# The last two blocks' attention divided in SBUF, and late outputs that sum their experts in one bank

## The chip, the core and the metric

The kernel runs on one core of one Trainium2 chip. The metric is the device time of one execution in microseconds, and the median of three executions stands for a kernel. Beside them there is one profiled execution, whose trace gives the time of every instruction. The engines are called PE (matmuls; PEld is its weight load), DVE (vector), ACT (scalar activation), POOL (GpSimd) and SP, which here only issues DMA transfers. Each engine works its own queue of instructions strictly in the order in which the program put them there.

## What is computed

The input is four images of 128 channels and 64x64 pixels, that is 4 x 4096 tokens of 128 channels. Two layers follow one another. The first normalises, convolves, runs a Mamba scan (16 states for each of 4 x 4 channel groups) and projects. The second is what the change is about:

```python
def _L1_attn_ref(x, W_qkv, b_qkv, W_proj, b_proj):
    # E = 128 channels, H = 4 heads of D = 32
    ...
    scores = jnp.einsum('bhnd,bhmd->bhnm', q, k) * scale
    att = jax.nn.softmax(scores, axis=-1)
    out = jnp.einsum('bhnm,bhmd->bhnd', att, v)
    out = jnp.transpose(out, (0, 2, 1, 3)).reshape(b, n, e)
    return out @ W_proj + b_proj

def _L1_ffn_ref(x, router_w, router_b, expert_w, expert_b):
    # E = 8 experts, K = 2 of them for each token
    router_probs = jax.nn.softmax(x @ router_w + router_b, axis=-1)
    top_p, top_i = jax.lax.top_k(router_probs, K)
    top_p = top_p / jnp.sum(top_p, axis=-1, keepdims=True)
    expert_out = jnp.einsum('bnd,edc->bnec', x, expert_w) + expert_b
    gathered = jnp.take_along_axis(expert_out, top_i[..., None], axis=2)
    return jnp.einsum('bnk,bnkc->bnc', top_p, gathered)

t = t + _L1_attn_ref(_ln_t(t), ...)
t = t + _L1_ffn_ref(_ln_t(t), ...)
```

## The kernel before

The work is cut into blocks of 512 tokens, eight for each of the four images. The program is one long loop over slots (from line 1362). Each pair of slots of the first 1024 takes one unit of the scan; `END` (line 1340) is the slot behind the last unit. In every slot there is also one step of attention, called a group, if one is ready: four score matmuls, two exponentials on ACT, and, one slot later, eight matmul calls that add the weighted values to the bank `av` (`weighted`, line 981). A matmul of fp32 operands is recorded twice in the trace.

Attention goes by pairs of blocks of queries: `q` is a pair, `u` one block of it. For each head `h` of a pair all keys of the image are run through, in pieces that `RUNS` (line 903) orders; the last piece of every image is the whole of pair 3. When the last group of a head's piece is done, `avs` takes the bank out to SBUF (a copy on ACT, or an addition of `prev`, the partial sum of earlier pieces, on DVE). It holds two blocks: partitions 64u to 64u+31 are the head's 32 output channels, not yet divided, and partitions 64u+32 to 64u+63 repeat the softmax denominator.

If the head is final, `avs` is sent to the DRAM tensor `total` (line 1007). Behind the fourth head `inverted` (line 1012) loads the denominators of all heads as `den`, 128x32, takes the reciprocal, and sends it to the DRAM tensor `inverse`; then it queues two tasks "out", one for each block. These three steps come 4, 6 and 8 slots after the fourth head.

A task "out" is `finished` (line 1032), a generator that does the rest of a block. Each `yield` ends one stage. It loads `aT` (the undivided attention, four heads on 128 partitions), `inv` (the reciprocals, repeated for the 32 channels of a head) and `acc` (the block's residual) from DRAM, multiplies aT by inv on DVE (line 1047), projects with `wp` on PE, adds to `acc`, takes the norm's statistics, transposes, computes the routing with some 20 small DVE instructions, and sends the shares of the eight experts to DRAM as `shares`. From there `share` (line 1117) loads them again, two experts at a time, repeated over all partitions. DVE multiplies the tokens by the shares and PE multiplies by the experts' weights. The bias of the experts and each two experts make a bank of their own; DVE adds it to `res` in SBUF (lines 1134, 1145 and 1152), so that there are five additions for one block.

Two lanes of such tasks, X and Y, run beside attention. `advance` (line 1254) carries a lane on by one stage; in a slot the calls come in the order X, Y, Y, X, the last X behind `weighted`. Up to `END` lane Y prepares the scan's blocks and lane X does the closing of blocks and the outputs. From `END` on lane Y takes outputs from lane X's list as well (line 1261), so they go in pairs. Each lane has one PSUM bank. `send` (line 422) issues a transfer some slots later on SP. All engine instructions of the loop go through `queued` (line 389), which chains them in program order; for this reason every profile line reads L406, and groups are told apart by the tiles they name.

Of the kernel before, what the change touches and what calls it, by code (L numbers as in the profile page):

```python
# [9 lines left out]
F32 = mybir.dt.float32  # L10
# [7 lines left out]
P = 128  # L18
C = 128
EPS = 1e-5  # L20
BLK = 512
# [4 lines left out]
DH = 32  # L26
NH = 4
NE = 8
# [8 lines left out]
def conv_mamba_attn_moe_kernel(ctx: ExitStack, tc: tile.TileContext, t: dict):  # L37
    nc = tc.nc
    x, out = t["x"], t["out"]
    B, _, L = x.shape  # L40
    NB = L // BLK
# [41 lines left out]
    wv, wp, rw, ew, eb8 = (load(k, eng=late) for k in ("wv", "wp", "rw", "ew", "eb8"))  # L83
# [13 lines left out]
    for j in range(4):  # L97
        r = slice(DI * (j % 2), DI * (j % 2) + DI)
# [301 lines left out]
    class Queue:  # L400
# [7 lines left out]
    tensor, vector, scalar, gpsimd, sync = (  # L408
        Queue(e) for e in (nc.tensor, nc.vector, nc.scalar, nc.gpsimd, nc.sync)
    )  # L410

    def mm(out, lhsT, rhs, start=True, stop=True):
        tensor.matmul(out, lhsT=lhsT, rhs=rhs, start=start, stop=stop)
# [8 lines left out]
    def send(out, in_, slots=1):  # L422
        outgoing.append([slots, out, in_])
# [19 lines left out]
    att, mix, side = pool("att"), pool("mix"), pool("side")  # L443
# [4 lines left out]
    def work(lane, shape=None):  # L448
        return ps_work.tile(shape or [P, BLK], F32, tag=f"work{lane}", name=f"ps_{lane}")

    def tmp(lane, name, shape=None):
        return side.tile(
            shape or [P, BLK], F32, tag=f"tmp{lane}", name=name, bufs=6 if lane == "X" else 4
        )
# [516 lines left out]
    sums, partial, total, inverse, later = [None], {}, {}, {}, deque()  # L971
# [9 lines left out]
    def weighted(group):  # L981
        b, q, h, pTs, first, last, prev, final = group
        if first:
            sums[0] = ps_av.tile([P, BLK], F32, name="av")
        av = sums[0]
        for k, (v, pT) in enumerate(pTs):
            for u in range(2):
                mm(
                    av[64 * u : 64 * u + 2 * DH, :], v, pT[:, u, :],
                    first and k == 0, last and k == STEP - 1,  # L990
                )
        if last:
            avs = att.tile([P, BLK], F32, name="avs", bufs=2)
            if prev is None:
                scalar.copy(avs, av)
            else:
                vector.tensor_add(avs, av, prev)


            if not final:  # L1000
                partial[b, q, h] = dram.tile([P, BLK], F32, name=f"avd{q}{h}")
                send(partial[b, q, h], avs, 3)
                return
            if h == 0:
                total[b, q] = dram.tile([2, 2, NH, DH, BLK], F32, name=f"total{q}")
            d = total[b, q]
            send(d[:, :, h].rearrange("u k r q -> (u k) r q"), avs, 3)
            if h == NH - 1:
                work_left = inverted(b, q)
                later.extend((slot + n, work_left) for n in (4, 6, 8))  # L1010

    def inverted(b, q):

# [15 lines left out]
            ))  # L1029
        yield  # L1030

    def finished(b, qb, lane):

        q, u = divmod(qb, 2)
        td = kqv[b][3]
        s = slice(qb * BLK, (qb + 1) * BLK)
        acc = side.tile([P, NT, C], F32, name="acc", bufs=2)
        aT, inv = tmp(lane, "aT"), tmp(lane, "inv")
        sync.dma_start(out=aT, in_=total[b, q][u, 0].rearrange("h d q -> (h d) q"))
        sync.dma_start(  # L1040
            out=inv, in_=inverse[b, q][u][:, None, :].to_broadcast([NH, DH, BLK])
        )
        sync.dma_start(out=acc.rearrange("p j c -> p (j c)"), in_=td[:, s])
        yield
        yield
        yield
        vector.tensor_mul(aT, aT, inv)
        yield
        ps = work(lane, [P, NT, C])
        for j in range(NT):  # L1050
            mm(ps[:, j, :], aT[:, j * P : (j + 1) * P], wp)
        yield
        vector.tensor_add(acc, ps, acc)
        rs = spread(lane, acc)
        yield
        ps = transposed(lane, acc)
        yield
        xf = tmp(lane, "xf")
        scalar.copy(xf, ps)
        yield  # L1060
        ps = work(lane, [P, NT, NE])
        for j in range(NT):
            mm(ps[:, j, :], xf[:, j * P : (j + 1) * P], rw)
        wide = [P, NT, NE]

        def routed(name, n=NE):
            return small.tile([P, NT, n], F32, name=f"{name}{lane}", bufs=1)

        yield

        both = routed("both", 2 * NE)
        pr = routed("pr")
        vector.tensor_mul(pr, ps, rs[:, :, None].to_broadcast(wide))
        vector.tensor_add(pr, pr, rb[:, None, :].to_broadcast(wide))
        m = routed("m", 1)
        vector.tensor_reduce(m, pr, AX.X, ALU.max)
        vector.tensor_sub(pr, pr, m.to_broadcast(wide))
        yield
        yield
        scalar.activation(pr, pr, AF.Exp)  # L1080
        yield
        yield

        revb = rev[:, None, :].to_broadcast(wide)

        def largest(src, tag):
            top, f, pick = routed(f"top{tag}", 1), routed(f"f{tag}", 1), routed(f"pick{tag}")
            vector.tensor_reduce(top, src, AX.X, ALU.max)
            vector.tensor_tensor(pick, src, top.to_broadcast(wide), ALU.is_equal)
            vector.tensor_mul(pick, pick, revb)  # L1090
            vector.tensor_reduce(f, pick, AX.X, ALU.max)
            vector.tensor_tensor(pick, pick, f.to_broadcast(wide), ALU.is_equal)
            return top, pick

        top1, pick1 = largest(pr, 1)
        rest = routed("rest")
        vector.scalar_tensor_tensor(rest, pick1, -2.0, pr, ALU.mult, ALU.add)
        top2, pick2 = largest(rest, 2)
        vector.tensor_add(pick1, pick1, pick2)
        vector.tensor_mul(pr, pr, pick1)  # L1100
        vector.tensor_add(top1, top1, top2)
        vector.reciprocal(top1, top1)
        vector.tensor_mul(both[:, :, 0:NE], pr, top1.to_broadcast(wide))
        vector.tensor_mul(both[:, :, NE:], both[:, :, 0:NE], rs[:, :, None].to_broadcast(wide))
        yield

        ps = work(lane)
        for j in range(NT):
            tensor.transpose(ps[0 : 2 * NE, j * P : (j + 1) * P], both[:, j, :], ident)
        yield  # L1110
        prT = tmp(lane, "prT")[0 : 2 * NE, :]
        scalar.copy(prT, ps[0 : 2 * NE, :])
        shares = dram.tile([NE, BLK], F32, name=f"shares{lane}")
        send(shares, prT[NE:, :])
        yield

        def share(e):

            if lane == "X":
                w = side.tile([P, 2, BLK], F32, name="share", bufs=3)  # L1120
            else:
                w = mix.tile([P, 2, BLK], F32, tag="rows", name="share", bufs=4)
            sync.dma_start(
                out=w.rearrange("p k q -> p (k q)"),
                in_=shares[e : e + 2].rearrange("e q -> (e q)")[None].to_broadcast([P, 2 * BLK]),
            )
            return w


        ps = work(lane)  # L1130
        mm(ps, eb8, prT[0:NE, :])
        yield
        res = tmp(lane, "res")
        vector.tensor_add(res, ps, xf)
        yield
        ahead = deque(share(e) for e in (0, 2))
        yield
        yield
        for e in range(0, NE, 2):
            if e + 4 < NE:  # L1140
                ahead.append(share(e + 4))
            yield
            w = ahead.popleft()
            if e:
                vector.tensor_add(res, res, ps)
            vector.tensor_mul(w, w, xf[:, None, :].to_broadcast([P, 2, BLK]))
            yield
            ps = work(lane)
            for u in range(2):
                mm(ps, ew[:, e + u, :], w[:, u, :], u == 0, u == 1)  # L1150
        yield
        vector.tensor_add(res, res, ps)
        send(out[b][:, s], res, 2)
        yield

# [94 lines left out]
    lanes, done, running = {"X": deque(), "Y": deque()}, set(), {}  # L1250
# [50 lines left out]
    X, Y = lanes["X"], lanes["Y"]  # L1301
# [9 lines left out]
    for k in range(-2, len(blocks)):  # L1311
        if 0 <= k:
            b, i = blocks[k]
            Y.append((("in", b, i, 1), inputs(b, i, 1), [("scan", *blocks[k - 1], 1)] if k else []))
        if k + 2 < len(blocks):
            b, i = blocks[k + 2]
            if k + 2 == 0 or i > 0:
                upper(k + 2)
        if 0 <= k + 1 < len(blocks):
            b, i = blocks[k + 1]  # L1320
# [19 lines left out]
    END = 2 * len(units)  # L1340

    rows, due, closing, y_of = {}, deque(), deque(), {}
    h_of, slot = {}, 0
# [18 lines left out]
    while (  # L1362
# [13 lines left out]
        if unit and not odd:  # L1376
            h = h_of.pop(at)
# [44 lines left out]
    with tc.If(nc.values_load(general[0:1, 0:1]) > 0):  # L1422
# [4 lines left out]
        with tc.For_i(0, B, 1) as b:  # L1427
# [3 lines left out]
                out=t_tok.rearrange("p k c -> p (k c)"),  # L1431
                in_=tsave[bass.ds(b, 1)].rearrange("o p q -> (o p) q"),
            )
            with tc.tile_pool(name="ps_again", bufs=4, space=PSUM) as psum:
                for i in range(NB):
                    ps = anew(t_tok[:, NT * i : NT * (i + 1), :], psum)
# [92 lines left out]
```

## Times and the profile before

| what | value |
|---|---|
| median of three runs | 5179.66 us (5176.39 to 5188.5) |
| profiled execution | 5183.13 us, of which the span from first to last instruction is 5180.9 us |
| PE busy over the span | 4710.1 us, 91% |
| DVE busy | 3835.8 us, 74% |
| ACT busy | 3745.7 us, 72% |
| chain that ended last, by engine | PE 59%, DVE 19%, ACT 10%, DMA 6% |
| aT products with inv on DVE | 32, mean 690 ns |
| additions to res from a bank, 128x512 | 160 in all, mean 683 to 691 ns |

A row of busy time says how long an engine worked, and not whether anything waited for it. Which step counts is read from the chain of work that ended last: it begins at the last instruction and follows back, at each step, what released it. In a timeline each row gives start, duration, engine, line, operation, output and inputs, and in brackets the idle time before it with what ended it.

### The profile page before, as it was taken

What the parts mean: (1) busy time and instruction counts of PE and PEld (TensorE: products, weight loads), DVE (VectorE), ACT (ScalarE), POOL (GpSimd) and SP (SyncE); (2) the same over time, 40 slices, a digit from 0 to 9 for tenths busy, and PEclk for the clock granted to TensorE, in tenths of its full rate; (3) what the DMA queues carried; (4) which work ended last, traced back from release to release, by engine and by line L of the source; (5) the groups of instructions that cost most, each with busy time, mean ns of one, the idle gap of its engine ahead of it and who ended that gap; (6) DMA issues with size and microseconds to landing.
All of it is one profiled execution on the core that took longest, in us unless ns stands there. A gap on an engine that the chain in (4) does not pass through costs nothing.

```text
span 5180.9 us, 62597 instructions
## 1 busy us (share of the span) xinstructions
PE 4710.1 (91%) x20684; PEld 2321.9 (45%) x20684; DVE 3835.8 (74%) x5780; ACT 3745.7 (72%) x5700; POOL 423.1 (8%) x483
## 2 busy tenths in 40 slices
PE   4567898999999998899999999999999999999997
PEld 2334444444444444444444444444444444443443
DVE  6987767877778887878788887888788877751332
ACT  4556777787787787688888787788777787656543
POOL 1111111100000000101000000000000001000000
PEclk7778999999999999899999999999999999999998
DMA  3556667677666766767766766777766666754542
GB/s 127 183 186 212 205 212 253 233 239 243 229 224 225 239 227 234 242 230 258 252 228 227 238 229 231 258 231 255 265 227 233 221 230 221 262 179 156 184 134 72
DMA packets 451693, 1131.70 MB, mean 218 GB/s; under 512 B 51858, under 2 KB 135331, under 8 KB 451363
## 3 DMA queue, kind: packets, MB, share of 16 engines
q1 hardware_dynamic: 447296, 1125.96, 64.3%
q8 instruction: 166, 2.72, 0.2%
q10 hardware_dynamic: 4066, 1.67, 0.1%
q14 instruction: 165, 1.34, 0.1%
HBM read 967.22 MB, written 143.39 MB: 214 GB/s over the span
## 4 chain that ended last, share of the span: by engine, by line
PE 59%; DVE 19%; ACT 10%; DMA 6%; issue 4%; POOL 2%; SPq 1%; DVEq 0%; ACTq 0%; POOLq 0%
PE av L406 25%; PE sc L406 14%; PE ps_X L406 9%; DVE h L406 6%; PE ps_Y L406 6%; PE y L406 5%; ACT pT L406 3%; ACT L406 2%; DVE hc L406 2%; DMA ks<-kd 2%; ACT xt L406 1%; DVE stX L406 1%; DVE du L406 1%; DMA rows<-bcd 1%; DVE cm L406 1%
## 5 line engine op out<-in xcount | busy, mean ns | idle before, releaser
L406 ACT ACTIVATE pT<-sc 128x1024 f32<-128x1024 f32 x2048 | 1984.3, 1022 | 934.3 <-PE sc L406 932.8
L406 PE MATMUL av<-pT,v 128*64 128x512 f32 x8192 | 2002.8, 610 | 10.8 <-DVE avs L406 10.8
L406 PE MATMUL sc<-qs,ks 128*128 128x512 f32 x4096 | 1302.7, 437 | 75.9 <-ACT pT L406 39.4
L406 DVE TENSOR_TENSOR_SCAN h<-da,state,h 128x1025 f32<-128x1025 f32 x512 | 1204.5, 2353 | 96.6 <-ACT h L406 62.8
L406 PEld LDWEIGHTS sc<-qs,ks 128*128 128x128 f32 x4096 | 703.1, 190 | 812.7 <-ACT pT L406 273.2
L406 PEld LDWEIGHTS av<-pT,v 128*64 128x64 f32 x8192 | 500.4, 137 | 845.7 <-issue 816.7
L406 ACT ACTIVATE da<-delta,amat 128x512 f32<-128x512 f32 x1024 | 742.9, 730 | 1.9
L406 PE MATMUL y<-ident,hc 128*128 128x128 f32 x4096 | 626.2, 284 | 64.6 <-DVE hc L406 64.6
L406 DVE TENSOR_TENSOR hc<-rows,h 128x1024 f32<-128x1024 f32 x512 | 624.6, 1220 | 15.3 <-PE y L406 5.4
L406 DVE TENSOR_TENSOR h<-rows,du 128x1024 f32<-128x1024 f32 x512 | 623.9, 1218 | 13.0 <-DMA rows<-bcd 8.5
L406 PEld LDWEIGHTS y<-ident,hc 128*128 128x128 f32 x4096 | 524.2, 147 | 229.0 <-issue 80.8
L406 ACT ACT_TABLE_LOAD x319 | 409.3, 1283 | 19.5 <-DVE zs L406 14.3
L406 POOL TENSOR_TENSOR rsX<-rsX,mhalf 128x4 f32<-128x4 f32 x92 | 203.7, 2214 | 2504.4 <-DVE rsX L406 2420.4
L406 POOL TENSOR_TENSOR rsY<-rsY,mhalf 128x4 f32<-128x4 f32 x100 | 130.7, 1307 | 2072.5 <-DVE shiftY L406 1561.5
L406 DVE TENSOR_TENSOR avs<-av,prev 128x512 f32<-128x512 f32 x96 | 66.2, 689 | 256.7 <-PE av L406 235.0
L406 PE MATMUL ps_X<-share,w_ew 128*128 128x512 f32 x432 | 213.9, 617 | 9.1 <-DVE share L406 8.8
L406 ACT ACTIVATE xt<-ps_Y,shiftY,rsY 128x128 f32<-128x128 f32 x380 | 143.6, 468 | 81.7 <-POOL shiftY L406 73.8
L406 DVE TENSOR_TENSOR share<-share,xf 128x1024 f32<-128x1024 f32 x128 | 156.0, 1219 | 16.5 <-DMA share<-sharesX 11.7
L406 ACT COPY state<-h 128x2 f32<-128x2 f32 x448 | 88.8, 198 | 92.0 <-DVE h L406 92.0
L406 DVE SCALAR_TENSOR_TENSOR cm<-y,w_fc1w,cm 128x512 f32<-128x512 f32 x195 | 145.1, 744 | 8.0 <-ACT y L406 4.5
L406 PE MATMUL ps_Y<-pairs,inxc 128*128 128x512 f32 x256 | 132.6, 643 | 15.5 <-DMA pairs<-xn 9.9
L406 PEld LDWEIGHTS ps_X<-share,w_ew 128*128 128x128 f32 x432 | 73.2, 189 | 147.0 <-issue 97.1
(248 smaller groups left out, 3437.2 us busy)
## 6 DMA issues: line engine op xcount, KB each, us to landing
rows<-bcd SPq DMA_DIRECT2D x1024, 512.0 KB
ks<-kd SPq DMA_DIRECT2D x192, 512.0 KB
qs<-qd SPq DMA_DIRECT2D x161, 512.0 KB
share<-sharesX SPq DMA_DIRECT2D x108, 512.0 KB
v<-vd SPq DMA_DIRECT2D x192, 256.0 KB
ks<-kd SPq DMA_DIRECT2D x128, 256.0 KB
avd<-avs SPq DMA_DIRECT2D x96, 256.0 KB
prev<-avd SPq DMA_DIRECT2D x96, 256.0 KB
```

Of the source, the lines that this page charges most:

```text
L406: return lambda *args, **kw: queued(op(*args, **kw))
```

## The change

There are two parts. First, for the last pair of blocks of the last image (`b == B - 1 and q == NB // 2 - 1`) a final head does not go to `total`. A new function `divided` takes the reciprocal of the whole of `avs` (128x512) and multiplies, for each of the two blocks, the head's 32 partitions by the reciprocals of its denominator into 32 partitions of a tile `quotient[u]`. Its buffers are those of `xin` and `prev`. Behind the fourth head the two tasks "out" are put at the end of lane X's list at once, and `finished` gets the quotient as `aT`; it then neither loads aT and inv nor passes through the four stages with the product. To make this possible the load of `acc` is moved ahead of those of aT and inv, for all blocks.

Second, for outputs whose expert stage begins at `END` or later (`one`) the expert biases and all eight experts accumulate in one PSUM bank, and DVE adds the bank to the tokens once, at the end.

```diff
+            if b == B - 1 and q == NB // 2 - 1:
+                divided(b, q, h, avs)
+                return
             d = total[b, q]
             send(d[:, :, h].rearrange("u k r q -> (u k) r q"), avs, 3)
...
+    quotient = []
+
+    def divided(b, q, h, avs):
+
+        if h == 0:
+            quotient.extend(mix.tile([P, BLK], F32, name="xin", bufs=2) for _ in range(2))
+        rec = att.tile([P, BLK], F32, name="prev", bufs=2)
+        vector.reciprocal(rec, avs)
+        for u in range(2):
+            r, d = 64 * u, 64 * u + DH
+            vector.tensor_mul(
+                quotient[u][DH * h : DH * h + DH, :], avs[r : r + DH, :], rec[d : d + DH, :]
+            )
+        if h == NH - 1:
+            for u in range(2):
+                lanes["X"].append((
+                    ("out", b, 2 * q + u),
+                    lambda lane, i=2 * q + u, a=quotient[u]: finished(b, i, lane, a), [],
+                ))
...
-    def finished(b, qb, lane):
+    def finished(b, qb, lane, aT=None):
...
-        aT, inv = tmp(lane, "aT"), tmp(lane, "inv")
-        sync.dma_start(out=aT, in_=total[b, q][u, 0].rearrange("h d q -> (h d) q"))
-        sync.dma_start(
-            out=inv, in_=inverse[b, q][u][:, None, :].to_broadcast([NH, DH, BLK])
-        )
         sync.dma_start(out=acc.rearrange("p j c -> p (j c)"), in_=td[:, s])
-        yield
-        yield
-        yield
-        vector.tensor_mul(aT, aT, inv)
-        yield
+        if aT is None:
+            aT, inv = tmp(lane, "aT"), tmp(lane, "inv")
+            sync.dma_start(out=aT, in_=total[b, q][u, 0].rearrange("h d q -> (h d) q"))
+            sync.dma_start(
+                out=inv, in_=inverse[b, q][u][:, None, :].to_broadcast([NH, DH, BLK])
+            )
+            yield
+            yield
+            yield
+            vector.tensor_mul(aT, aT, inv)
+            yield
         ps = work(lane, [P, NT, C])
...
-        mm(ps, eb8, prT[0:NE, :])
+        mm(ps, eb8, prT[0:NE, :], True, slot < END)
         yield
-        res = tmp(lane, "res")
-        vector.tensor_add(res, ps, xf)
+        one = slot >= END
+        if not one:
+            res = tmp(lane, "res")
+            vector.tensor_add(res, ps, xf)
...
-            if e:
+            if e and not one:
                 vector.tensor_add(res, res, ps)
             vector.tensor_mul(w, w, xf[:, None, :].to_broadcast([P, 2, BLK]))
             yield
-            ps = work(lane)
+            if not one:
+                ps = work(lane)
             for u in range(2):
-                mm(ps, ew[:, e + u, :], w[:, u, :], u == 0, u == 1)
+                mm(
+                    ps, ew[:, e + u, :], w[:, u, :], u == 0 and not one,
+                    u == 1 and (not one or e + u == NE - 1),
+                )
         yield
-        vector.tensor_add(res, res, ps)
+        if one:
+            res = tmp(lane, "res")
+            vector.tensor_add(res, ps, xf)
+        else:
+            vector.tensor_add(res, res, ps)
         send(out[b][:, s], res, 2)
```

## The prediction

> **What bounds the kernel now.** I read the busy times by stretch first, for the time after the scan's end (the last scan work is near 4580 us), then the chain of work that ended last, then the timeline around single steps. Columns of the first: stretch, its length, then PE, PEld, DVE, ACT, POOL busy (with counts), the granted PE clock, DMA share, GB/s.
>
> ```profile
> 4812.00:4880.00 68.00, 63.00 (x246) 28.76 (x248) 31.28 (x86) 28.07 (x33) 2.02 (x2) 0.97 0.60 199
> 4880.00:4946.00 66.00, 65.16 (x263) 29.23 (x260) 29.68 (x84) 30.61 (x36) 2.01 (x2) 1.00 0.42 146
> 5012.00:5115.00 103.00, 103.00 (x417) 39.70 (x415) 0.69 (x1) 67.08 (x70) 0.00 (x0) 1.00 0.21 67
> 5115.00:5181.00 66.00, 30.26 (x86) 14.88 (x84) 29.10 (x83) 3.36 (x7) 2.01 (x2) 0.70 0.31 102
> ```
>
> Up to 5115 PE has almost no idle time: attention fills it and pairs of outputs (one in lane X, one in lane Y, near 4600, 4820, 4885 and 4952) run in between. From 5115.3 there is no attention left, and the last pair runs alone for 66 us, with PE busy less than half of it. That tail is a chain of latencies:
>
> ```profile
> 5115.39 0.59 ACT avs L406
> 5116.00 5.82 DMA total<-avs
> ...
> 5122.47 2.00 DMA den<-total
> 5124.49 0.36 DVE den L406
> 5124.87 1.41 DMA inverse<-den
> ...
> 5127.85 8.68 DMA inv<-inverse
> ...
> 5136.62 0.70 DVE aT L406
> ...
> 5153.26 3.88 DMA share<-sharesY
> 5157.17 1.24 DVE share L406
> 5158.45 3.57 PE ps_Y L406 x4
> ```
>
> So four dependent transfers stand between the last head's sums and its product with the reciprocal denominators, and 20 us pass before the second lane's projection.
>
> **What the skill says.** (1) "VectorE: DVE Perf Modes", section "First, the fixed hardware budget": reciprocal is an iterative divide with a repeat count of 8. The trace agrees that it is slow per element, at some 6 ns (below) against 1.04 for an addition. (2) The same page, section "Two Vector instructions with no wait between them": an instruction whose operands start in another group of 32 partitions than its predecessor's waits until that has finished. So I let the new products overlap with nothing; no row of before shows such a pair. (3) "TensorE: Matmul & The Clock Gate", section "Part 1: The HAM clock gate": after an idle window of about 3.4 us the clock is halved, until a busy window has passed. The trace agrees: eight projection records take 2.08 us behind a 4.09 us gap at 4817 and 1.16 us at 4821.6. (4) "DMA: Bandwidth & Descriptors", section "Anatomy of one DMA": about 2 us fixed per transfer, measured there for transfers that GpSimd issues; here SP does. The chain's four took 5.8, 2.0, 1.4 and 8.7 us; the measured ones are used.
>
> **Part 1: the division of the last pair, in SBUF.** It removes the transfers `total`, `den`, `inverse`, `aT`, `inv` and one aT product per lane. It adds for each of four heads one reciprocal of 128x512 and two products of 32x512. Their prices:
>
> ```profile
> L406 DVE RECIPROCAL den<-den 128x32 f32<-128x32 f32 x16 | 5.5, 345 | 111.7 <-DMA den<-total 111.7
> L406 DVE RECIPROCAL top1X<-top1X 128x4 f32<-128x4 f32 x27 | 4.8, 178 | 0.9
> L406 DVE TENSOR_TENSOR aT<-aT,inv 128x512 f32<-128x512 f32 x32 | 21.8, 690 | 66.1 <-DMA inv<-inverse 60.7 <-issue 5.4
> ```
>
> From 4 to 32 elements the reciprocal grows by (345-178)/28 = 5.96 ns each, with 154 ns fixed: 154 + 512 x 5.96 = 3.21 us, an estimate. Lower bound: 0.69, if it ran like an addition. Upper: the page's 8 repeats at the addition's 1.04 ns, 0.15 + 512 x 8.3 = 4.4 us. I take 3.21, since two rows of the same operation give it. A product of 32 partitions costs as one of 128, 0.69 (ACT's copies show that partitions are free: 0.57 for 16x512, 0.59 for 128x512).
>
> Call A = 5115.98 the end of the avs copy. The first quotient is ready at A + 3.21 + 0.69 + 0.08 for two handovers = A+4.0, the second 0.7 later. `acc` is loaded long before, since its issue stands behind the last values on SP and waits for nothing. Lane X goes first now. Its projection takes 1.1 us at full clock, 2.1 at half; its acc addition starts at A+5.15 or A+6.1. The other lane's acc addition follows on DVE after addition, statistics and scale of the first, 2.08 us (before: 5137.23 to 5139.31), so at A+7.2 or A+8.2. In before that second addition starts at 5139.49 = A+23.5. From there both kernels do the same work with the lanes exchanged. Gain 16.3 or 15.3; whether a whole idle window falls into the 4.6 us gap is chance, so **-15.8**. If the reciprocal hits its bounds: -18.3 to -14.6.
>
> Heads 0 to 2 divide earlier. For heads 1 and 2 DVE is empty (0.69 us busy from 5012 to 5115) and nobody waits: nothing, for that reason alone. Head 0 is different. It ends inside the pair near 4950, and in the changed order of instructions its reciprocal and two products stand between the two lanes' aT products:
>
> ```profile
> 4946.15 1.29 DVE L406 TENSOR_TENSOR aT<-aT,inv 128x512 f32<-128x512 f32 x2
> 4951.35 0.59 ACT L406 COPY avs<-av 128x512 f32<-128x512 f32 x1 [0.35 <-PE av L406]
> 4952.27 1.05 PE L406 MATMUL ps_Y<-w_wp,aT 128*128 128x128 f32 x8
> 4955.12 1.16 PE L406 MATMUL ps_X<-w_wp,aT 128*128 128x128 f32 x8
> ```
>
> Before, both aT were ready 5 us early. Now DVE waits for avs until 4951.94; reciprocal to 5 hundredths after + 3.21 = 4955.2, products to 4956.65, lane X's aT to 4957.4. Behind it queue both acc additions, and PE, in order, waits with lane X's projection from 4955.12 to 4957.4, and attention behind that: **+2.3**, with nothing hiding it, as PE is full until the end (bounds: 0 and 3.5). Lane Y's acc is added by 4958.1 and needed at 4959.3, so nothing else is late.
>
> **Part 2: acc's load goes ahead of aT and inv**, for the 30 other outputs too. On SP it costs half a microsecond of issue, and 256 KB stand ahead of inv in the queues. In the tail three such loads (acc, aT, inv) separate the two landings of inv, 5132.46 and 5136.58: 4.1/3 = 1.4 us each. Where inv ends a wait on the path, that is 1.4 late: the gap of 4.09 us ahead of the projection at 4817 (**+1.4**), and one place of the chain in the middle, 12 us of inv from 1298.5 (**+1.4**). DVE waits for inv in 16 of the 22 outputs before 4580, but PE then waited 0.2 us at most for aT, twice, and works off attention meanwhile: nothing for these; if the cover is gone, 1.4 each. Together 0 to 6.
>
> **Part 3: one bank for the experts.** Per output four additions of 0.69 us go, in ten outputs. In the four pairs among attention this is hidden: a step there takes 6.43 us (4857.58 to 4864.01), namely attention 2.99 and two experts of two products 2 x 1.72, all PE. So nothing. In the tail the last 32 records ran from 5158.45 to 5175.44, 17.0 us. Without the additions between them DVE needs 8 x 1.13 = 9 us, and PE is the limit: the first four cold 3.57, then 7 x 1.72 = 12.0, so 15.6. Gain 1.4, less some for the landing of the second lane's shares (5160.4 in before): **-1.2** (0 to -1.6). The last addition (0.69) and the output's store (4.7) stay.
>
> **Sum.** -15.8 + 2.3 + 2.8 - 1.2 = -11.9. The profiled execution took 5183.13 (span 5180.9 and 2.2 around it): 5171.2. Its time is 3.5 above the median of the runs, so 5179.66 - 11.9 = **5167.8**.
>
> **Rivals.** *The reciprocal takes 8 cycles an element.* For: the page. Against: the two rows. +1.2 in the tail, +1.2 at head 0: 5170.2. *It runs at an addition's pace* on long rows: -2.5 and -2.3: 5163.0; against it, the same rows. *The additions were on the path in the four pairs*, because PE's ends are modelled and its busy records could hide waits: 32 x 0.69 = 22 us: 5145.7; against it, the step that is exactly the sum of its matmuls. *The load order decides:* each of the 22 outputs before the scan's end has its aT product 1.4 us later, DVE stands in order ahead of the scan, and if every delay reaches PE that is 30.8 in place of 1.4: 5197.2, slower. It outweighs the gain from some ten such outputs on (13.3 / 1.4 = 9.5). For: DVE's 16 waits; against: one chain entry in 22.
>
> **Chances.** Main case 0.62 (own range 5161 to 5174: load order 0 to 6, clock phase, head 0); 8 cycles 0.14; fast reciprocal 0.08; additions on the path 0.07; load order 0.09. The range 5159 to 5176 leaves out the last two and a few per cent of the others. A measurement of this kernel tells about 0.2% from no change, 10.4 us, that is 5169.3. The forecast lies just below: two thirds of the main case (0.41), half of the 8 cycles (0.06) and both faster rivals give 0.61 faster; slower 0.07, most of the load-order case; 0.32 within.
>
> **What would show it.** RECIPROCAL of 128x512 near 3.2 us; the tail from the end of avs to the second acc addition 7 to 8 us, formerly 23.5; lane X's projection near 4955 with some 2.3 us of wait for aT; PE's gap near 4817 a little over 5 us; expert products in the tail at 1.7 to 1.8 per four; no fewer microseconds between 4857 and 4880. I am wrong if the stretch before 4800 moves by more than 5 us, or if PE's idle time in the pairs was more than the trace shows.

## The result and the profile after

| | kernel before | changed kernel |
|---|---|---|
| median of the runs, taken side by side | 5179.38 us (5172.48 to 5190.66, 16 runs) | 5169.68 us (5160.33 to 5180.86, 16 runs) |
| ratio of the times | | 0.9983, 95% interval 0.9976 to 0.9990 |
| profiled execution: span | 5180.9 us | 5172.0 us |

The change saves 9.7 us by the medians, 8.9 us between the two profiled spans; forecast were 11.9. That is 0.19%, at the edge of what can be told from no change, but the interval lies wholly on the faster side.

Where the microseconds went is read by laying marks into both traces. Marks 1 to 4 are the starts of lane X's first transpose of `bothX` in the four pairs of outputs that run among attention; A is, as in the prediction, the end of the last `avs` copy.

| section of the trace | before | after | difference |
|---|---|---|---|
| start to mark 1 | 4615.77 | 4617.13 | +1.36 |
| mark 1 to mark 2 (holds the gap near 4817) | 225.61 | 226.84 | +1.23 |
| mark 2 to mark 3 | 66.73 | 66.73 | 0 |
| mark 3 to mark 4 (holds head 0's division) | 66.53 | 70.54 | +4.01 |
| mark 4 to A (heads 1 and 2) | 141.34 | 141.33 | -0.01 |
| A to the end (the tail) | 64.92 | 49.43 | -15.49 |

The sum is -8.9. The first row says nothing: in all kernels measured here mark 1 lies between 4605.6 and 4625.8. The rows behind it come to -10.3. They can be compared, since they hardly move where nothing was changed; only the second also moves with how long PE's clock is halved behind the gap (see the load order below).

Busy times by stretch of the changed kernel, with the columns explained in the prediction:

```profile
4812.00:4880.00 68.00, 62.72 (x246) 28.04 (x243) 25.26 (x77) 28.60 (x34) 2.01 (x2) 0.95 0.56 191
4880.00:4946.00 66.00, 65.16 (x264) 29.04 (x262) 24.51 (x76) 31.28 (x36) 2.01 (x2) 1.00 0.43 154
4946.00:5012.00 66.00, 63.04 (x251) 28.95 (x249) 27.81 (x76) 29.93 (x35) 2.01 (x2) 0.97 0.36 128
5012.00:5121.00 109.00, 109.00 (x435) 42.46 (x435) 10.82 (x8) 69.02 (x72) 0.00 (x0) 1.00 0.20 65
5121.00:5172.00 51.00, 30.42 (x90) 15.56 (x86) 27.03 (x75) 3.36 (x7) 2.01 (x2) 0.70 0.27 95
```

The reader is to see three things. In the first two stretches DVE lost some 6 and 5 us of work (31.28 and 29.68 before), and PE, the bound, kept its 62.7 and 65.2. From 5012 to 5121 DVE got 10 us more and PE is still full. And the last stretch, the tail, is 51 us long where it was 66, with the clock at 0.70 as before.

DVE's timeline at the head of the tail, changed kernel:

```profile
5122.59 3.35 DVE L406 RECIPROCAL prev<-avs 128x512 f32<-128x512 f32 x1 [41.84 <-ACT avs L406]
5125.98 1.41 DVE L406 TENSOR_TENSOR xin<-avs,prev 32x512 f32<-32x512 f32 x2
5128.84 0.69 DVE L406 TENSOR_TENSOR acc<-ps_X,acc 128x512 f32<-128x512 f32 x1 [1.45 <-PE ps_X L406]
...
5130.82 0.69 DVE L406 TENSOR_TENSOR acc<-ps_Y,acc 128x512 f32<-128x512 f32 x1
```

And PE's:

```profile
5126.72 2.08 PE L406 MATMUL ps_X<-w_wp,xin 128*128 128x128 f32 x8 [4.79 <-DVE xin L406]
5128.59 1.91 PE L406 MATMUL ps_Y<-w_wp,xin 128*128 128x128 f32 x8
...
5149.37 3.78 PE L406 MATMUL ps_X<-share,w_ew 128*128 128x512 f32 x4 [2.52 <-DVE share L406]
5152.94 2.91 PE L406 MATMUL ps_Y<-share,w_ew 128*128 128x512 f32 x4
5155.69 1.88 PE L406 MATMUL ps_X<-share,w_ew 128*128 128x512 f32 x4
```

A is 5122.57. No transfer stands between A and the projections any more: reciprocal, products, 4.79 us of idle PE, two projections. The second addition to `acc` starts at A+8.25, formerly at A+23.51. Both projections run at half clock (2.08 and 1.91 for eight records, against 1.16 at full clock), and so do the first expert products.

The prices of the new instructions, from the groups of the changed kernel:

```profile
L406 DVE RECIPROCAL prev<-avs 128x512 f32<-128x512 f32 x4 | 13.4, 3352 | 98.8 <-ACT avs L406 98.8
L406 DVE TENSOR_TENSOR xin<-avs,prev 32x512 f32<-32x512 f32 x8 | 5.5, 684 | 0.2
```

PE's waits from 4690 to the end (for whom, sum, times, longest), changed kernel:

```profile
PE ps_X L406 <- DVE xin L406: 4.8, 1, 4.8
PE ps_Y L406 <- DVE aT L406: 4.6, 1, 4.6
...
PE ps_X L406 <- DVE aT L406: 2.3, 1, 2.3
```

Before, the wait of lane Y's projection for aT came to 22.0 us in two parts, 17.9 of them in the tail. The 17.9 are gone, 4.8 stand in their place, the gap near 4817 (4.6) has stayed, and a wait of 2.3 is new. It is the one at head 0:

```profile
4953.94 0.59 ACT L406 COPY avs<-av 128x512 f32<-128x512 f32 x1 [0.35 <-PE av L406]
4954.56 3.35 DVE L406 RECIPROCAL prev<-avs 128x512 f32<-128x512 f32 x1 [5.13 <-ACT avs L406]
...
4957.94 1.38 DVE L406 TENSOR_TENSOR xin<-avs,prev 32x512 f32<-32x512 f32 x2
4959.35 0.69 DVE L406 TENSOR_TENSOR aT<-aT,inv 128x512 f32<-128x512 f32 x1
...
4960.10 1.78 PE L406 MATMUL ps_X<-w_wp,aT 128*128 128x128 f32 x8 [2.33 <-DVE aT L406]
...
4961.54 2.05 PE L406 MATMUL sc<-qs,ks 128*128 128x512 f32 x4
```

This timeline of the changed kernel shows the wait of 2.33 us at the length forecast. It also shows what was not forecast: behind it the projection takes 1.78 in place of 1.16, and the four score records 2.05 in place of 1.17. The clock was halved here too.

### The profile page after: what moved, and what is told of

It reads as the page before. It is cut to its first block, busy times and chain, and to the rows that moved or that the text cites. A ratio compares the mean times of both kernels' runs of the same rounds, so it can differ in the third digit from the quotient of the medians.

```text
span 5172.0 us, 62513 instructions
## 1 busy us (share of the span) xinstructions
PE 4712.2 (91%) x20684; PEld 2324.6 (45%) x20684; DVE 3825.9 (74%) x5749; ACT 3746.5 (72%) x5700; POOL 423.0 (8%) x483
```

## The experiments

The theory after the result: the division in SBUF brings the whole gain; part of it is given back at head 0, where a wait of 2.3 us costs 4.0 because PE comes out of it at half clock; the load order and the one bank are worth about a microsecond each, with opposite signs. The rivals: that the one bank carries part of the gain; that the load order costs much more, before the scan's end; that the extra 1.7 us at head 0 come from somewhere else than the clock. None of the kernels leaves work out; `e6_head0_twice` takes one reciprocal twice, and those with a function `warm` add 15 matmuls whose results nobody reads.

### Each part alone

`e1_division_only` is the changed kernel with the experts summed as before:

```diff
-        mm(ps, eb8, prT[0:NE, :], True, slot < END)
+        mm(ps, eb8, prT[0:NE, :])
...
-        one = slot >= END
+        one = False
```

> The first part alone: quotients in SBUF and the load of acc ahead of aT and inv, experts summed in five banks with additions as before. My theory: the gain of the change is the division, so the time stays within 1.5 us of the changed kernel (about 5170), the tail from the end of the last avs copy to the end of the span is 49 to 51 us, and the step between attention and experts in the pairs near 4860 stays at 6.43 us. Rival (the additions were on the path in the four pairs and in the tail): about 7 us slower than the changed kernel or more.

Measured: ratio 0.9985 (0.9977 to 0.9993), span 5171.5, second addition to `acc` at A+8.27, mark 3 to 4 70.49, tail 50.68. The division alone brings what the whole change brings (0.9983).

`e2_bank_only` is the kernel before with the second part of the change alone:

```diff
-        mm(ps, eb8, prT[0:NE, :])
+        mm(ps, eb8, prT[0:NE, :], True, slot < END)
...
+        one = slot >= END
...
-                mm(ps, ew[:, e + u, :], w[:, u, :], u == 0, u == 1)
+                mm(
+                    ps, ew[:, e + u, :], w[:, u, :], u == 0 and not one,
+                    u == 1 and (not one or e + u == NE - 1),
+                )
...
```

> The second part alone: one bank for the experts from the scan's end on, division and load order as before. My theory: within 0 to 1.5 us below the kernel before (about 5179), the tail 63 to 65 us against 64.9, PE without change in the four pairs. Rival (additions on the path): 20 us faster.

Measured: ratio 0.9994 (0.9986 to 1.0003), second addition at A+23.77, the expert products from first to last 16.96 us where before has 16.99, and mark 2 to 3 66.74. The interval includes no change. The tail is 66.48 us, longer than before (64.92) and outside the 63 to 65 expected: the half clock lasts without a break from 5108.23 to 5156.02 in this execution, so that eight routing records take 1.71 us in place of 0.98. That the additions had been on the path in the four pairs, with 22 us to win, falls: the pairs take the same time to a few hundredths with and without them.

### Head 0

`e3_head0_later` divides head 0 together with head 1, when DVE is empty:

```diff
-        rec = att.tile([P, BLK], F32, name="prev", bufs=2)
-        vector.reciprocal(rec, avs)
+        undivided.append((h, avs))
+        while h and undivided:
+            k, avs = undivided.pop(0)
+            rec = att.tile([P, BLK], F32, name="prev", bufs=2)
+            vector.reciprocal(rec, avs)
...
```

> The changed kernel, but head 0 is divided together with head 1, behind the pair of outputs near 4950 and not inside it. My theory: the 2.33 us in which PE waited for lane X's product and the half clock that followed both go, so PE takes 66.5 us from the wait for bothX near 4910 to the next near 4975, in place of 70.5, and the whole is 4 us faster than the changed kernel (about 5166). Rival 1 (only the wait counts, the clock would have dropped anyway): 68.2 us there, 2.3 us faster. Rival 2 (the two reciprocals behind one another at head 1 hold up something else): no gain.

Measured: ratio 0.9967 (0.9954 to 0.9980), mark 3 to 4 66.55, mark 4 to A 141.33, tail 49.11. PE's timeline at the same place, in this kernel:

```profile
4947.88 1.05 PE L406 MATMUL ps_Y<-w_wp,aT 128*128 128x128 f32 x8
4948.86 1.94 PE L406 MATMUL av<-pT,v 128*64 128x512 f32 x8
4950.73 1.16 PE L406 MATMUL ps_X<-w_wp,aT 128*128 128x128 f32 x8
```

There is no bracket at lane X's projection, so PE did not wait, and it runs at full clock. By time alone this kernel isn't told from the changed one, whose interval (0.9976 to 0.9990) overlaps; by the marks it is. The whole +4.0 between marks 3 and 4 came from head 0's division, and moving it costs nothing elsewhere: three heads in the empty stretch are as free as two.

`e5_head0_part` and `e6_head0_twice` change the dose. The first divides 384 of head 0's 512 columns there and the rest with head 1, the second takes head 0's reciprocal twice:

```diff
# e5_head0_part
-        vector.reciprocal(rec, avs)
+        parts = [(h, avs, 0, 384 if h == 0 else BLK)]
+        if h == 1:
+            parts.append((0, undivided.pop(), 384, BLK))
+        for k, a, c0, c1 in parts:
...
+            vector.reciprocal(rec[:, c0:c1], a[:, c0:c1])
...
# e6_head0_twice
-        vector.reciprocal(rec, avs)
+        for _ in range(2 if h == 0 else 1):
+            vector.reciprocal(rec, avs)
```

> The changed kernel, but of head 0 only 384 of the 512 columns are divided inside the pair near 4950, the other 128 with head 1. With 6.26 ns per element the stay of PE ahead of lane X's projection falls from 2.33 to about 1.26 us. My theory (a short gap does not halve the clock, the 1.67 us above the wait at 2.33 are the clock's): PE takes 66.53 + 1.26 = 67.8 us between the bothX steps near 4910 and 4975. Rival 1 (any gap costs the 1.67 us again): 69.5. Rival 2 (the 1.67 us are not the clock but instructions that queue in DVE behind the division, in proportion to its length): about 68.7.

> The changed kernel, but the reciprocal of head 0 is computed twice, so that PE waits 5.7 us in place of 2.33. My theory (wait plus one or two windows of half clock of 1.7 us each): 74 to 75.7 us between the bothX steps, in place of 70.5. Rival 2 (in proportion to the division, 4.0 per 2.33): 76.3 or more. The end moves by as much, 3.4 to 5.2 us.

Measured in one execution each (5175.13 and 5182.77 us), read from the marks. PE's timeline of `e5_head0_part`:

```profile
4963.11 1.16 PE L406 MATMUL ps_X<-w_wp,aT 128*128 128x128 f32 x8 [1.26 <-DVE aT L406]
4964.02 1.18 PE L406 MATMUL sc<-qs,ks 128*128 128x512 f32 x4
```

and of `e6_head0_twice`:

```profile
4968.30 2.08 PE L406 MATMUL ps_X<-w_wp,aT 128*128 128x128 f32 x8 [5.72 <-DVE aT L406]
4970.02 2.05 PE L406 MATMUL sc<-qs,ks 128*128 128x512 f32 x4
```

| wait of lane X's projection | kernels | mark 3 to 4, against 66.53 | granted clock behind the wait, in stretches of 2 us |
|---|---|---|---|
| 0 | e3, e8 | 0.0 | 1.00 |
| 1.26 | e5 | +1.33 | 1.00 |
| 2.33 | changed kernel, e1, e4, e7 | +3.95 to +4.01 | 0.61, then 0.53 (changed kernel) |
| 2.33 | e9 (below) | +2.40 | 1.00 |
| 5.72 | e6 | +7.91 | 0.50, 0.50, 0.77 |

The records of the granted clock say more. In all 13 traces the clock takes only the values 1 and one half, and it changes only at instants that lie on a grid of 3.41 us, to within 0.004 us; the place of the grid differs from execution to execution. A step of the grid is called a window here. In the changed kernel the whole wait (4957.77 to 4960.10) fell into one window, and the next was at half clock (the clock is the third number from the right):

```profile
4957.04:4960.45 3.41, 1.08 (x7) 0.35 (x4) 3.33 (x5) 0.00 (x0) 0.00 (x0) 1.00 0.00 0
4960.45:4963.86 3.41, 3.41 (x15) 2.92 (x14) 3.27 (x20) 1.02 (x2) 1.01 (x1) 0.50 0.02 5
```

In `e9_warm_five_banks`, where the wait is just as long, a window's edge cut it into 1.95 and 0.38 us, and the clock stayed:

```profile
4962.34:4965.75 3.41, 1.46 (x8) 0.29 (x4) 3.33 (x4) 0.28 (x1) 0.00 (x0) 1.00 0.01 2
4965.75:4969.17 3.42, 3.04 (x20) 2.37 (x22) 3.32 (x15) 1.32 (x2) 1.01 (x1) 1.00 0.02 5
```

With the clock at 1.00 the same wait of 2.33 costs 2.40, and with the clock halved 4.0. So the wait's own price is its length, as forecast, and the other 1.6 to 1.7 us are the half clock behind it: a window of 3.41 us at half clock loses half of itself, 1.7 us, of a full PE (an estimate). In `e1_division_only`, `e4_load_order` and `e7_warm_tail` the wait also lay in one window, and the next was at half clock. So whether such a wait meets the half clock hangs, as far as these five executions show, on the grid's place, which is chance; no run here sets it on purpose.

### The load order

`e4_load_order` is the changed kernel with the old order of loads, except that `acc` is still loaded for the last pair:

```diff
-        sync.dma_start(out=acc.rearrange("p j c -> p (j c)"), in_=td[:, s])
-        if aT is None:
+        whole = aT is None
+        if whole:
             aT, inv = tmp(lane, "aT"), tmp(lane, "inv")
...
+        sync.dma_start(out=acc.rearrange("p j c -> p (j c)"), in_=td[:, s])
+        if whole:
             yield
...
```

> The changed kernel with the load of acc behind those of aT and inv again, for the 30 outputs that load them. My theory: PE's gap ahead of the projection near 4817 goes from 4.65 back to about 4.1 us and the DVE waits for inv before the scan's end are shorter by half a microsecond each, of which PE feels 1 us at most: 0.5 to 1.5 us faster than the changed kernel. Rival (each delay of the scan reaches the end): 10 us faster or more.

Measured: ratio 0.9973 (0.9965 to 0.9980), which overlaps the changed kernel's 0.9983 (0.9976 to 0.9990); the middles are 5 us apart. PE's gap near 4817 is 3.84 us in it, 4.65 in the changed kernel, but mark 1 to 2 is 226.80, as in the changed kernel (226.84).

`e11_acc_first` is the reverse, the kernel before with nothing changed but `acc` loaded first:

```diff
+        sync.dma_start(out=acc.rearrange("p j c -> p (j c)"), in_=td[:, s])
         aT, inv = tmp(lane, "aT"), tmp(lane, "inv")
...
-        sync.dma_start(out=acc.rearrange("p j c -> p (j c)"), in_=td[:, s])
```

> The kernel before with only the load of acc moved ahead of those of aT and inv. My theory: PE's gap near 4817 grows by half a microsecond, the pairs otherwise take what they took, and the time is 0 to 3 us above the kernel before, which a measurement cannot tell from none. Rival (every output's delay reaches the end): 10 us slower or more.

Measured: ratio 1.0008 (1.0000 to 1.0016), that is 0 to 8 us slower, the middle 4. Its gap near 4817 is 4.35, and mark 1 to 2 is unchanged at 225.62. The four kernels with the old order and this gap (the kernel before, `e2_bank_only`, `e4_load_order`, `e8_all_three`) have 4.09, 3.86, 3.84 and 4.42; the eight with the new order lie between 4.35 and 4.86. The means are 4.05 and 4.64, some 0.6 apart.

This longer gap hardly shows in mark 1 to 2. What that mark follows is the number of half-clock windows behind the gap: with one it lies between 225.60 and 226.42 (the kernel before, `e2_bank_only`, `e3_head0_later`, `e5_head0_part`, `e8_all_three`, `e9_warm_five_banks`, `e11_acc_first`), with two between 226.80 and 227.46 (the changed kernel, `e1_division_only`, `e4_load_order`, `e6_head0_twice`, `e7_warm_tail`), and each group has kernels of both orders. Within a group the orders are 0.2 us apart in the mean (226.01 and 225.77 with one window, 227.03 and 226.80 with two). The +1.23 between the first two profiles compares a kernel with one such window to a kernel with two, so it can't be put down to the load order.

DVE's waits of the aT products for inv come to 72.1 us over the whole run here, 60.7 before; and to 58.7 in the changed kernel, 45.4 with the old order in it. So the order costs DVE 11 to 13 us over some 22 outputs before the scan's end, half a microsecond each, and most of that is covered. That every delay reaches the end (30.8 us, the slower rival) falls. Whether the 4 and 5 us between the middles are real, and where in the first 4600 us they would arise, isn't settled: the scatter of mark 1 is larger than they are.

### The half clock in the tail, and what one bank is worth without it

`e7_warm_tail` fills PE's idle time in the last pair with 15 matmuls of 128x512 in four places (ahead of lane X's projection, behind lane Y's routing, behind lane X's transposes, behind lane Y's bias product). Everything else is as changed:

```diff
+    def warm(n):
+        sc = ps_sc.tile([P, 2, BLK], F32, name="sc")
+        for k in range(n):
+            mm(sc[:, k % 2, :], ident, taps.rearrange("p k q -> p (k q)")[:, 0:BLK])
...
+        alone = b == B - 1 and q == NB // 2 - 1
+        if alone and lane == "X":
+            warm(5)
...
```

> The changed kernel with 15 matmuls of 128x512 added to PE in the gaps of the tail (five behind the last attention, four and two around the routing, four ahead of the experts); their results go into score banks that nobody reads. My theory (PE's half clock costs the tail about 1 us ahead of the second acc addition and 2 in the experts): second acc addition at A+7.2 in place of A+8.25, experts' matmuls about 15 us from first to last in place of 16.8, the tail 46 to 47 us in place of 49.4, the whole 2.5 to 3.5 us faster than the changed kernel. Rival (the tail hangs on DVE and the transfers, the clock is hidden): no gain, or slower by what the added matmuls keep PE busy.

Measured: ratio 0.9969 (0.9958 to 0.9980), second addition at A+7.35, expert products 15.47 us from first to last, tail 46.56. PE's timeline of this kernel:

```profile
5118.24 4.56 PE L406 MATMUL sc<-taps,ident 128*128 128x512 f32 x10
5123.10 1.16 PE L406 MATMUL ps_X<-w_wp,xin 128*128 128x128 f32 x8 [0.30 <-DVE xin L406]
...
5144.40 1.98 PE L406 MATMUL ps_X<-share,w_ew 128*128 128x512 f32 x4 [0.68 <-DVE share L406]
5147.59 1.98 PE L406 MATMUL ps_Y<-share,w_ew 128*128 128x512 f32 x4 [1.20 <-DVE share L406]
5149.41 1.88 PE L406 MATMUL ps_X<-share,w_ew 128*128 128x512 f32 x4
5151.12 1.88 PE L406 MATMUL ps_Y<-share,w_ew 128*128 128x512 f32 x4
```

The projection takes 1.16 and the first expert products 1.98 (3.78 in the changed kernel). The half clock of the tail was worth 49.43 - 46.56 = 2.9 us: 0.9 ahead of the second addition, 1.3 in the expert products, and the rest between and behind. By the whole time alone this kernel isn't told from the changed one, whose interval overlaps; the tails of `e3_head0_later`, `e5_head0_part` and `e6_head0_twice`, which have the changed kernel's tail, took 49.1 to 49.6, so the 2.9 are well outside that scatter. (`e4_load_order` has the same tail too and took 51.32: the shares of its second lane landed late, DVE waited 3.07 us for them, and its expert products took 19.20.)

`e9_warm_five_banks` is `e7_warm_tail` with the experts summed as before:

```diff
-        mm(ps, eb8, prT[0:NE, :], True, slot < END)
+        mm(ps, eb8, prT[0:NE, :])
...
-        one = slot >= END
+        one = False
```

> The changed kernel with the added matmuls in the tail, but the experts in five banks with the additions between them, so that the second part is priced at full clock. My theory: the experts' matmuls take 16.5 to 17 us from first to last in place of 15.1 to 15.5 with one bank, so the second part is worth 1 to 1.5 us when the clock is full. Rival (DVE's additions hide in the waits for the shares): the same 15.1 to 15.5.

Measured in one execution (5178.31 us): 16.53 us from first to last expert product, all at full clock, tail 49.51. Only 1.06 of the 2.9 us by which this tail is longer than that of `e7_warm_tail` lie there: in this execution the clock was halved from 5136.42 to 5143.24, in spite of the added matmuls, and the experts began 1.2 us later, counted from A. DVE's timeline of this kernel:

```profile
5158.56 0.69 DVE L406 TENSOR_TENSOR res<-res,ps_Y 128x512 f32<-128x512 f32 x1 [0.34 <-PE ps_Y L406]
5159.16 1.22 DVE L406 TENSOR_TENSOR share<-share,xf 128x1024 f32<-128x1024 f32 x1
5160.30 0.68 DVE L406 TENSOR_TENSOR res<-res,ps_X 128x512 f32<-128x512 f32 x1
5160.90 1.22 DVE L406 TENSOR_TENSOR share<-share,xf 128x1024 f32<-128x1024 f32 x1
5162.46 0.69 DVE L406 TENSOR_TENSOR res<-res,ps_Y 128x512 f32<-128x512 f32 x1 [0.34 <-PE ps_Y L406]
```

Two groups of experts (one in each lane) repeat every 5162.46 - 5158.56 = 3.90 us, 1.95 each, where PE alone needs 1.71 (5149.41 to 5151.12 in `e7_warm_tail`). Addition and product take turns with the matmuls. One bank takes that out: 15.47 in `e7_warm_tail`, 15.07 in `e8_all_three` and 15.52 in `e10_later_product`, against 16.53, so 1.0 to 1.5 us. In the changed kernel itself little of it is seen, 16.79 against 16.99, because its first two groups ran at half clock (3.78 and 2.91). The windows show why. First the kernel before, then the changed kernel, from the window in which the first expert product starts:

```profile
5158.24:5161.65 3.41, 3.20 (x4) 1.18 (x4) 1.35 (x2) 0.00 (x0) 0.00 (x0) 0.50 1.03 382
5161.65:5165.07 3.42, 3.22 (x8) 1.36 (x8) 3.05 (x5) 0.00 (x0) 0.00 (x0) 1.00 0.93 335
```

```profile
5148.18:5151.60 3.42, 2.23 (x3) 1.17 (x4) 1.62 (x2) 0.00 (x0) 0.00 (x0) 0.50 1.02 398
5151.60:5155.01 3.41, 3.41 (x5) 1.30 (x4) 3.41 (x4) 0.00 (x0) 0.00 (x0) 0.50 0.85 322
```

Before, the first product (5158.45) came 0.2 us behind a window's edge, PE was busy for 3.20 us of that window, and the next was at full clock. In the changed kernel it came (5149.37) 1.18 us behind an edge, PE was busy for 2.23 us, and one more window passed at half clock.

### All together, and one step further

`e8_all_three` puts `e3_head0_later`, `e4_load_order` and `e7_warm_tail` together:

```diff
+        undivided.append((h, avs))
+        while h and undivided:
...
+        sync.dma_start(out=acc.rearrange("p j c -> p (j c)"), in_=td[:, s])
+        if whole:
...
+        if alone and lane == "X":
+            warm(5)
...
```

> The changed kernel with head 0 divided with head 1, the load of acc behind those of aT and inv for the other outputs, and the added matmuls in the tail. If the three are independent: 4.0 for head 0, 0.5 to 1 for the load order and 2.5 to 3.5 for the clock, so 7 to 8.5 us faster than the changed kernel and 16 to 18 faster than the kernel before, a ratio near 0.9967. Rival (the gaps are shared, what one gives the other takes): no better than the run with head 0 later.

Measured: ratio 0.9968 (0.9956 to 0.9979), near the 0.9967 forecast. Both local gains are there, mark 3 to 4 at 66.52 and the tail at 46.48, but the whole can't be told from `e3_head0_later` (0.9967) or `e7_warm_tail` (0.9969): the differences are smaller than the intervals.

`e10_later_product` is `e8_all_three` with aT's product some two slots later for outputs behind the scan's end, to close the gap near 4817, which all kernels so far have:

```diff
-            yield
-            yield
-            yield
+            for _ in range(7 if slot >= END else 3):
+                yield
             vector.tensor_mul(aT, aT, inv)
```

> As the run of all three, and outputs from the scan's end on pass four more stages (two slots) before the product with inv, so that PE has attention queued ahead of their projection. My theory (the gap near 4817 is PE in order behind a late inv, and nothing needs these outputs soon): PE's gap of 4.4 to 4.7 us and the half clock behind it go, PE takes about 220 us from the first pair's bothX to the second's, less the two slots of attention moved (that is, last avs copy minus first bothX falls by 5 to 7 us), and the whole is 5 to 7 us faster than the run of all three. Rival (inv comes later still, or the later pairs push into the tail): no gain there, or a tail longer by some 6 us.

Measured: 5163.59 us, ratio 0.9956 (0.9943 to 0.9969), the lowest of all, and its interval lies wholly below that of the changed kernel. It overlaps that of `e8_all_three`, so the 5 to 7 us forecast between these two aren't shown by the whole time. PE's timeline at the place of the gap:

```profile
4812.90 1.19 PE L406 MATMUL sc<-qs,ks 128*128 128x512 f32 x4
4813.93 1.05 PE L406 MATMUL ps_Y<-w_wp,aT 128*128 128x128 f32 x8
4814.91 1.94 PE L406 MATMUL av<-pT,v 128*64 128x512 f32 x8
```

and in the changed kernel:

```profile
4819.28 2.08 PE L406 MATMUL ps_Y<-w_wp,aT 128*128 128x128 f32 x8 [4.65 <-DVE aT L406]
4821.28 1.98 PE L406 MATMUL av<-pT,v 128*64 128x512 f32 x4
```

The wait of 4.65 us is gone, with the half clock behind it (1.05 in place of 2.08 for the projection, and 1.94 for eight records of `av` where four took 1.98). Mark 1 to 2 falls from 226.10 in `e8_all_three` to 220.40. Both hold 64 slots of attention. Behind it the pairs stand later against attention: 2 to 3 and 3 to 4 are 72.52 and 72.51 with 17 slots each, formerly 15, and 4 to A is 124.55 with 35 slots, formerly 41. From mark 1 to A the kernel takes 10.7 us less (500.67 to 489.98), more than the 5 to 7 forecast; but it holds two slots less there, which run ahead of mark 1 (6.0 us at 2.99 a slot, an estimate), so 4.7 are won: the 5.7 of mark 1 to 2, less some 1 us behind mark 4. The tail is 47.45 in place of 46.48: here too the clock was halved for 6.83 us, from 5116.55 on.

## Why the forecast was right, and where its steps were off

| step | forecast | measured |
|---|---|---|
| reciprocal of 128x512 | 3.21 us (0.69 to 4.4) | 3.35 |
| second addition to `acc` | A+7.2 or A+8.2 | A+8.25 to A+8.27, in all six kernels with the division and no added matmuls |
| division of the last pair | -15.8 (-16.3 or -15.3) | -15.26 |
| heads 1 and 2, cover on DVE | 0 | mark 4 to A 141.34 and 141.33 |
| head 0 | +2.3 (0 to 3.5) | +4.0, of it 2.33 the wait |
| load order, gap near 4817 | +1.4 | gap 0.26 and 0.81 longer in the two pairs that differ in the order alone; mark 1 to 2 the same in both |
| load order, middle of the run | +1.4 | not told apart from scatter; the whole order 0 to 8 (`e11_acc_first`) |
| one bank in the tail | -1.2 (0 to -1.6) | -0.2 in the pair; -1.0 to -1.5 with PE at full clock |
| one bank in the four pairs | 0 | 0 |
| sum | -11.9 | -8.9 between the profiles, -9.7 by the medians |

**Right: what carries the gain.** The tail was a chain of latencies, and the four transfers in it were replaced by one reciprocal and two products. The addition's time at A+8.25 is the forecast's second branch, and `e1_division_only` shows that this step is the whole gain. The forecast treated the two branches as chance and took their middle; in fact the half clock came every time there, so -15.3 was the better number. The Trainium skill ("TensorE: Matmul & The Clock Gate", section "Part 1: The HAM clock gate") has the clock halved after an idle window of about 3.4 us. In the changed kernel no whole window was idle: an edge cut the gap of 4.79 us into 2.36 and 2.43, and the clock was halved all the same, at 5124.29. As 2.33 us in one window were enough at head 0, this gap can hardly escape: cut by one edge, it leaves at least half, 2.39 us, in one window (an estimate).

**Right: the price of the reciprocal.** The rows for 32 elements (345 ns, in the kernel before) and for 512 (3352) give (3352 - 345) / 480 = 6.26 ns an element; 5.96 had been read from the short rows. The rival of 8 additions' time per element and the one at an addition's pace are both out. The two products took 1.38 to 1.41 us, 684 ns each with no overlap, which agrees with the Trainium skill ("VectorE: DVE Perf Modes", section "Two Vector instructions with no wait between them").

**Mis-sized: head 0.** The step was "PE, in order, waits with lane X's projection from 4955.12 to 4957.4, and attention behind that: +2.3, with nothing hiding it". The mechanism was right, the wait was 2.33 us, and `e3_head0_later` takes it all away. The term that was too small is what follows the wait: the forecast put nothing for the clock there. In four of five executions with this wait PE came out of it at half clock for one window, for another 1.6 to 1.7 us. The page's idle window of about 3.4 us isn't what was measured: a stop of two thirds of a window was enough, where all of it fell into one. The bound of 3.5 is the wait with a reciprocal at its upper bound (3.21 to 4.4 us), and so missed 4.0.

**Mis-sized: one bank.** The forecast had the first four records cold (3.57) and the other seven groups at 1.72, 15.6 us. In the changed kernel the second group was cold too (2.91), which cost the microsecond that the edit gives. With the clock held up it gives it (1.0 to 1.5 us). The window merely fell so: the first product came 1.18 us behind a window's edge there and 0.2 behind it in the kernel before.

**Not borne out, or open: the load order.** For the gap near 4817 the forecast had +1.4, and mark 1 to 2 shows +1.23 between the first two profiles; that the two agree is luck, for a second window at half clock made the difference, which kernels of both orders have. In the two pairs that differ in the order alone the mark is the same within 0.04 us. Its second half, in the middle of the run, was never seen by itself. For the order as a whole `e4_load_order` and `e11_acc_first` leave 0 to 8 us, which holds the +2.8 and also almost nothing.

**The sum.** Between the two profiles it is 3.0 us short of the forecast. Head 0 (+1.7), one bank (+1.0) and the half clock ahead of the second addition (+0.5) make up that much. The +2.8 for the load order is matched by the +1.36 ahead of mark 1 and the +1.23 behind it, of which the first lies within scatter and the second is the clock's; that match is luck too.

## What to carry to other kernels

A chain of dependent transfers through DRAM at the end of a kernel, where no other work covers it, was worth replacing here even by a slow instruction on an idle engine: some 20 us of transfers went for a reciprocal of 3.35 us. But the same instruction put among full work costs its wait wherever the in-order queue of its engine stands ahead of the bounding one, so it has to be moved to where that engine is empty, as for head 0, which is 4 us here for a few lines. And a short wait of a full PE is to be priced with the half clock that may follow it, not by its length alone: here 2.33 us became 4.0 where the wait fell into one window. For the same reason a small difference between two profiles is to be compared with the clock of both before it is put down to the change.

## What the runs showed of the hardware

- The granted clock was 1 or one half, and changed only on a grid of 3.41 us, in all 13 traces; the grid's place differed between executions.
- A stop of PE of 2.33 us amid full load was followed by a window of half clock in the four executions where it fell into one window, and by none in the one where an edge cut it into 1.95 and 0.38 us; a stop of 1.26 us was followed by none (one execution), one of 5.72 by two windows (+2.2 us behind the wait, one execution).
- Fifteen matmuls of 128x512 that nobody reads, put into PE's idle time, took the tail from 49.43 to 46.56 us and the clock there from 0.70 to 0.99 (stretch 5116 to 5166 in `e7_warm_tail`). They didn't always hold the clock: in `e9_warm_five_banks` and `e10_later_product` it was halved for 6.83 us in the tail.
- The reciprocal on DVE costs 6.26 ns for each element of a partition, 3352 ns for 512 where an addition takes 690.
